# The first layer's mean and variance: from VectorE's statistics to two ScalarE passes

## The chip, the cores and the metric

The kernel runs on one core of a Trainium2 chip. Its time is the device time of one execution in microseconds. Three runs of the kernel before took 1981.17, 1981.98 and 1983.0 us; the median is 1981.98 us.

## The reference, cut to what matters

`x` has 128 batches of 128 rows (graph nodes) and 512 columns, in fp32, and `adj` is a 128 x 128 matrix. Four layers follow each other, and each ends in a layer norm over the 512 columns:

```python
def _layernorm(x, eps=1e-5):
    m, v = mean(x), var(x)          # over the 512 columns
    return (x - m) / sqrt(v + eps)

x = _layernorm(x + norm_adj @ x @ W0 + bias)                        # layer 0
x = _layernorm(x + L1(x, adj, adj, b))                              # layer 1
x = _layernorm(x + ((adj.T * (x Wq.T)(x Wk.T).T) / row norm) @ (x Wv.T))   # layer 2
h = x @ W3                                                          # layer 3
att = softmax(leaky_relu(s1 + s2.T) * adj)
x = _layernorm(x + elu(att @ h + beta * h))
```

Layer 1 is given the same matrix twice. With A equal to C - b, the maximum over all pairs adds to each row only a constant that its layer norm takes away, so that the kernel has no step for this layer's product; what is left of its norm is a factor for the variance of layer 0, `(1 + eps) * var + eps * eps`.

## The kernel before, in words

The work goes in 32 groups of four batches. A group's `x` is 128 rows by 4 x 512 columns. Per group there are these products on PE (all fp32): `y` (x transposed times the normalized adjacency, 16 matmuls), `w` (y times W0), `z` and `v` (x times Wq Wk and x times Wv), `r` (z times x), `f` (the masked relation times v), `k` (x times W3) and `h` (the attention times k). The products `w`, `z`, `v` and `k` use a scheme of seven block products instead of eight (class `Product`); some of the seven use it once more inside: these are first made in four small matmuls (for example step `z1`), then PE needs ACT to copy a part (`bz1`, `before`, L739) and DVE to add (`ez1`, `between`, L743), then come three more (`z18`). Others are added onto a PSUM bank after ACT has copied out what stood there (`cz1`, then `z6`; `cz6`, then `z7`).

The layer norms of layers 0, 2 and 3 are called `w`, `v` and `k`. For `v` and `k` the sum of a row comes with the last update of `x` on DVE; `mean` (L994) turns four sums into the two columns needed, `square_of` (L1000) is an ACT pass with a row sum of squares, `guard` (L1017) adds epsilon on ACT, `scale` (L1012) makes the power -1/2 on POOL, and `apply` (L1027) normalizes on ACT. For `w`, `stats` (L961) runs `bn_stats` and `bn_aggr` on DVE for each batch (steps `stw0` to `stw3`), and `guard` also negates the mean.

Left operands need transposed `x`. DVE transposes blocks of 32 (`xt`, `nt`: `square`, L670), then `xd` and `nd` move the blocks by 16 DMAs issued on SP (`exchange`, L676, issue at L680). The relation and the attention go through DRAM (`across`, L700): one DMA out (`wr`, `aw`), and four back (`cr`, `cat`). On POOL run the sums of left operands (`sy`, `sx`, `sn`: `Left.sum`, L613; the small ones `ly`, `lx`, `ln`: L631), the bias (`bi`, L955), the powers and parts of the softmax.

Everything is issued in an order written out by hand as three lists of step names, with a group number relative to a base: `HEAD` (L110) for the first groups, `TURN` (L258), which is repeated 14 times and moves on by a group each time, and `TAIL` (L275). Within an engine instructions run in the list's order. A turn has parts of six groups: for example group base + 4 is in its `w` product while base + 3 is in `z` and base + 1 in `k`. Buffers are chosen by the table `SLOTS` (L47): one digit for each tile that is made, for the six PSUM banks and the tags of SBUF tiles.

Of the kernel before, what the change touches and what calls it, by code (L numbers as in the profile page):

```python
# [38 lines left out]
AF = mybir.ActivationFunctionType  # L39
# [9 lines left out]
        "012345012345013324015345231455124240510435012532245312312023543413421402402052145230142402"  # L49
        "405233100340153013205320521340135305355234252351453524503210430454115310512125312305211451"  # L50
        "412523102304253042541105305015021541030340351405232432352315320142424230314525325435403451"
        "025252541243050250302310324152525234530121521015041053425252503201454254142134120352525210"
        "514323523435403451025252541243050250302310324152525234530121521015041053425252503201454254"
        "142134120352525210514323523435403451025252541243050250302310324152525234530121521015041053"
        "425252503201454254142134120352525210514323523435403451025252541243050250302310324152525234"
        "530121521015041053425252503043201513105140152035033042453510140541524513202020314220445020"
        "545523405212550033235143024014515313210213142055015354151041043201425125523020130023054354"
        "2045151501250312315415401340132145131523152403145324501324051324051"
    ),
    "S": (  # L60
        "012345601326054321502461532143250123654012106425231064104632501462035142560413524651203546"
        "413406524103561463205164231534062135410216534012605403216504352651403256124320651423046145"
        "320641563062145360231534062135410216534012605403216504352651403256124320651423046145320641"
        "563062145360231534062135410216534012631450326154036413652014326504152602324316052432560324"
        "152630645016325064152306"
    ),
    "l1": (
        "010111010101010010101011001101001011010010110100101101001011010010110100101101001011010010"
        "110100110010110011010110100100110"
    ),  # L70
    "l2": (
        "010101010101010010110110110110110110110110110110110110110110110110110110110110110101110101"
        "01"
    ),
    "C": (
        "010101010101011010101011011011011011011011011011011011011011011011011011011011011011011010"
        "10101010"
    ),
    "aT": (
        "012100212102102012012102012102012102012102012102012102012102012102012102012102102012012010"  # L80
        "2110210"
    ),
    "m": (
        "012301202302301210320100130133212013131201310310213231201012103232120131323021213103232120"
        "131323021213103232120131323021213103232120131323021213103232120131323021213103232120131323"
        "02121310233221302022132020213201210312121203210030"
    ),
    "x": (
        "0123457869789012345768901234576890123457689012345768901234576981032"
    ),  # L90
    "q": (
        "010101010101010001001010101010101010101010101011010101010101010100101010101001010101010101"
        "010101010101010001010101010101010101010101010101010101010101010101010101010101010101010101"
        "010101010101010101010101010101010101010101010101010101010101010101010101010101010101010101"
        "010101010101010101010101010101010101010101010101010101010100010101010101010101010101010101"
        "01010101010101010101010101010101010101010101010101010101010101010101010"
# [14 lines left out]
0.ld1 2.ld0 0.ld0 2.ld1 1.ld1 1.ld0 s.warm s.deg s.root s.nadj s.adjt s.nadjT 0.y10 0.y01 0.cy10  # L111
1.y10 0.cy01 1.y11 1.cy10 1.y01 1.cy11 0.y11 s.m012_0 1.cy01 3.ld1 s.s00 0.w2 s.m012_1 0.cy11
s.s02 0.bi10 s.m012_3 0.y00 0.bi01 2.y10 s.s01 0.cy00 2.y11 0.bi00 0.w1 s.m05_0 0.sy0 s.s03 2.y00
1.y00 0.bi11 s.m05_1 1.cy00 0.sy2 s.m012_2 0.w5 1.bi10 s.m05_3 0.sy3 0.dw1 s.m05_2 0.w6 0.sy1
0.dw2 s.sk0 1.ly12 s.sk2 s.g1 0.dw6 s.s30 0.w7 s.cg1 1.sy0 s.m312_0 1.bi11 0.dw7 s.m312_1 0.w4
1.bi00 0.dw5 s.bi 0.w3 s.sa1 2.cy10 0.dw4 2.cy00 s.sk1 2.cy11 s.g2 s.sa0 0.dw3 0.stw3 3.y11 1.bi01
0.stw0 s.g5 0.stw1 s.sa2 s.dg2 2.y01 s.s31 1.sy2 0.stw2 1.w2 2.cy01 s.s33 s.g6 0.gw s.sa3 1.bw2
s.m35_0 1.w1 s.cg6 0.pow 1.ew2 s.g7 1.bw1 s.m35_1 2.bi11 1.ew1 0.apw0 0.apw1 1.w28 0.xt0 1.ly5
1.w18 s.cg7 s.sk3 s.la 0.apw2 0.apw3 1.sy1 1.w5 1.dw1 3.ld0 0.xt2 s.g4 1.bw5 0.xt1 2.bi01 0.xt3
s.q11 1.w6 2.bi00 s.cg4 0.xd 1.ew5 s.mg12_0 3.bi11 1.w58 s.dg5 s.q02 s.g3 2.bi10 1.dw6 1.dw2 1.w7  # L120
s.dg3 2.ly12 s.mg12_1 1.dw7 s.mg12_3 1.w4 s.sg0 1.dw5 s.sg2 2.w2 s.sg1 4.ld0 2.w1 s.m312_3 2.bw2
s.sg3 2.ew2 2.bw1 0.z1 0.sx0 s.vt3 s.vt0 0.sx2 s.vt1 2.w28 0.cz1 1.dw4 1.sy3 s.vt2 0.z6 1.stw3
s.vd 0.sx1 1.stw2 1.w3 0.cz6 0.sx3 s.mg4_0 2.sy0 0.z5 2.ew1 1.dw3 2.sy1 0.z7 s.mg4_1 2.ly5 1.stw1
2.w18 s.mg4_3 0.cz7 0.z2 2.sy2 0.dz5 1.stw0 0.z4 0.dz2 1.gw s.mg5_0 s.mg12_2 1.pow s.mg5_2 0.z3
0.cz4 s.mg5_1 s.m35_3 1.apw3 s.mg5_3 3.y10 2.dw1 1.apw2 s.sv0 0.v1 1.apw0 3.bi10 2.dw2 1.apw1
1.xt2 s.sv1 0.v2 0.cv1 1.xt3 0.dz3 0.v6 1.xt0 0.dv2 1.xt1 0.r0 s.sv3 0.cv6 1.xd s.mv5_0 2.w5
s.mv4_0 s.mv5_1 s.mv4_1 s.sv2 0.r1 2.bw5 s.mv4_3 s.mv12_0 0.r2 2.ew5 0.r3 s.mv12_2 s.mv12_1 2.w58
s.mv5_3 s.mv12_3 0.rm 0.v7 s.q10 0.sq0 0.rt 0.sq1 2.w6 0.sq2 s.q12 0.cv7 s.q03 0.sq3 s.q00 0.rp
0.v4 s.q13 0.v5 3.cy11 s.q01 3.cy10 0.wr 2.dw6 0.cv4 4.ld1 3.sy0 s.wt0 s.s32 2.w7 2.sy3 0.cr 0.dv5
s.wt1 s.mv5_2 3.y00 1.sx0 2.dw7 0.v3 s.mg4_2 3.cy00 1.lx12 2.dw5 2.w4 s.mv4_2 0.dv3 0.f3 2.dw4  # L130
3.sy1 0.f1 2.stw2 0.f2 3.bi00 2.stw3 1.v1 0.fa3 1.lx4 0.fa2 1.z1 1.bv1 0.fa1 2.w3 1.bz1 1.ev1
1.lx5 1.ez1 0.f0 1.sx2 1.v5 2.dw3 0.fa0 1.z18 1.sx3 1.bv5 2.stw0 1.v18 0.mnv 1.cz1 1.ev5 1.z5
1.sx1 0.qv2 1.z6 2.stw1 0.qv1 1.cv1 0.qv0 1.z2 1.cz6 1.v6 1.bz2 0.qv3 1.ez2 1.bz5 1.z7 0.gv 2.gw
1.ez5 0.pov 1.cv6 2.pow 1.z28 0.apv3 1.z4 1.cz7 1.dz2 0.apv0 1.z58 0.nt3 2.apw0 1.v2 0.sc00 2.apw2
0.nt0 3.y01 1.bz4 0.sc01 0.apv2 1.v58 3.bi01 1.ez4 3.cy01 1.v7 0.apv1 0.nt2 3.ly5 2.apw1 0.sc10
1.bv2 1.z48 2.apw3 0.nt1 1.v4 1.cv7 3.ly12 1.dz4 0.nd 1.ev2 3.w5 1.bv4 1.dz5 1.v28 3.bw5 0.sc11
1.z3 3.ew5 1.dv2 3.w1 0.sc20 3.w2 1.dz3 3.bw1 0.sc21 3.w58 3.ew1 1.r0 1.r1 0.sc30 3.bw2 1.ev4 1.r2
1.r3 3.ew2 1.v48 0.sc31 3.w18 1.dv4 3.w28 0.pw 3.dw1 1.rm 0.k2 0.sn0 3.dw2 1.sq0 2.xt1 1.sq1 0.sn2
0.pe 2.xt0 0.k1 1.sq2 2.xt2 1.sq3 0.sn3 2.xt3 0.k5 1.rt 0.ck1 2.xd 1.rp 1.dv5 s.m312_2 0.sn1 0.pl3
0.dk2 1.v3 0.pl0 s.m35_2 0.pl1 0.pl2 3.sy2 0.k6 1.dv3 0.ej 3.w6 0.ck6 3.sy3 0.ei 0.ex0 0.k7 3.dw6  # L140
0.ex3 0.ex2 0.ex1 3.w7 0.rd 0.ck7 0.so0 0.dk5 0.so1 4.y11 3.dw7 1.wr 0.k4 3.dw5 4.bi11 0.at 0.aw
2.lx12 3.w4 4.cy11 1.cr 0.ck4 3.w3 3.dw4 2.sx0 3.stw2 0.cat 2.z1 3.stw3 2.sx2 2.z2 3.dw3 2.bz1
3.stw0 1.f2 2.sx1 2.bz2 3.stw1 2.v1 2.lx5 2.ez2 1.f0 3.gw 0.k3 1.fa2 2.bv1 3.pow 1.fa0 2.ez1 1.f1
2.lx4 3.apw0 0.dk3 1.f3 3.apw3 3.xt0 3.apw1 2.z18 1.fa1 3.apw2 0.h0 1.fa3 2.cz1 2.v5 3.xt2 1.mnv
3.xt1 0.h3 1.qv0 2.ev1 2.z28 1.qv1 2.z6 3.xt3 1.qv2 2.dz2 3.xd 1.qv3 0.em3 2.v18 0.em0 2.bv5 1.gv
0.h1 2.cz6 2.ev5 1.pov 0.ee0 2.z7 0.ee3 0.em1 1.apv3 0.ea0 1.apv0 0.ea3 2.v58 2.cz7 2.z5 1.sc00
0.ee1 1.apv1 4.y00 1.sc01 2.bz5 0.ea1 4.y10 1.apv2 4.bi00 2.ez5 4.cy00 4.y01 4.cy10 4.bi10 1.sc10
0.h2 4.cy01 1.sc11 2.z4 4.bi01 2.cv1 0.em2 2.v2 1.sc20 2.bz4 4.sy0 0.ee2 2.z58 2.ez4 2.bv2 2.v6
4.ly12 2.ev2 1.nt1 2.z48 2.cv6 1.sc21 2.v28 2.dz4 2.sx3 2.v7 1.sc30 3.sx0 2.dz5 4.w1 1.sc31 2.cv7
3.lx12 2.dv2 2.z3 1.pw 4.bw1 1.nt2 4.ew1 2.v4 2.dz3 1.pe 4.w18 3.sx2 1.nt0 2.bv4 2.r0 1.nt3 3.lx5  # L150
4.dw1 2.r1 2.ev4 3.z2 4.sy2 0.ea2 2.r2 1.pl3 1.pl0 2.r3 4.sy1 0.mnk 1.pl2 4.w6 1.pl1 3.sx1 2.rm
0.qk3 2.rt 2.sq0 1.ej 2.v48 0.qk2 2.wr 4.dw6 3.z1 2.dv4 1.nd 2.sq1 3.lx4 0.qk1 4.w7 1.ei 2.dv5
3.bz1 1.ex0 3.ez1 1.ex1 2.v3 1.ex3 4.sy3 1.ex2 4.dw7 2.sq2 3.bz2 1.rd 2.sq3 1.so0 3.z18 3.ez2
0.qk0 4.w4 3.sx3 3.cz1 2.dv3 0.gk 1.so1 3.z5 4.dw4 3.z6 0.pok 3.bz5 3.ez5 2.rp 0.apk3 3.z28 3.cz6
# [253 lines left out]
def kernel(  # L408
# [43 lines left out]
    def wide(t):  # L452
        return t.rearrange("p a b -> p (a b)")
# [954 lines left out]
```

## Time and profile before

| | |
|---|---|
| median of three runs | 1981.98 us |
| the profiled execution's own time | 1983.26 us |
| its span, first to last instruction | 1981.5 us |
| granted TensorE clock, mean | 0.998 |
| ACT passes of `square_of` (L1003) | 248, 721 to 722 ns each, and 188 ns for the row sum's read |
| ACT passes of `apply` (L1029) | 383, 808 ns each |
| `bn_stats` of `w` on DVE (L965) | 128, 677 ns each |
| 16 DMA issues of one `xd` or `nd` on SP | 10.7 to 12.3 us |

The page gives busy time by engine. PE is the matmuls and PEld the loading of their weights, DVE is VectorE, ACT ScalarE, POOL GpSimd, and SP issues the DMAs. A matmul of fp32 here leaves two records. In the chain of waits a row has a start, a length and what ran; in the groups by line, the two numbers after the first bar are busy microseconds and the mean nanoseconds of one, and after the second bar stands the idle time before them and what ended it.

### The profile page before, as it was taken

To read this page: it belongs to the slowest core of one execution; us is meant where nothing else is said; L and a number is where in the kernel's file an instruction comes from. 1 tells how busy PE (TensorE), PEld (TensorE's weight loads), DVE (VectorE), ACT (ScalarE), POOL (GpSimd) and SP (SyncE) were. 2 spreads that over 40 slices of the span, in tenths; PEclk is the share of its full clock that TensorE was granted. 3 is DMA by queue.
4 is the path that set the end of the run, shared out by engine and by line. 5 is a ranking of instruction groups with operands and counts; after the bars stand their busy time and mean duration, and the time that the engine had idled before them with its cause. 6 is when DMAs were issued, how large, how long until landed. Compare 5 with 4: busy or idle time off the path is not lost.

```text
span 1981.5 us, 37439 instructions
## 1 busy us (share of the span) xinstructions
PE 1954.1 (99%) x12405; PEld 1723.5 (87%) x12405; DVE 1645.2 (83%) x3801; ACT 1125.0 (57%) x2800; POOL 1372.1 (69%) x1702
## 2 busy tenths in 40 slices
PE   8999999999999999999999999999999999999997
PEld 7888988888888988888988888988889888898885
DVE  7888787888788888888888888888888888787887
ACT  2245556565655656565556556556656556566467
POOL 7557678676687776786766776766877767777652
PEclk9999999999999999999999999999999999999999
DMA  5523455334444345444345443445343454434434
GB/s 199 85 52 66 96 80 135 60 87 101 106 100 95 66 89 107 104 99 76 81 91 113 98 106 58 92 98 112 92 102 59 92 106 100 96 62 107 76 73 107
DMA packets 737312, 184.55 MB, mean 93 GB/s; under 512 B 689376, under 2 KB 689760, under 8 KB 737120
## 3 DMA queue, kind: packets, MB, share of 16 engines
q1 hardware_dynamic: 736976, 182.03, 43.7%
q8 instruction: 100, 1.64, 0.4%
q14 instruction: 92, 0.75, 0.1%
q10 hardware_dynamic: 144, 0.13, 0.0%
HBM read 64.03 MB, written 49.87 MB: 57 GB/s over the span
## 4 chain that ended last, share of the span: by engine, by line
PE 86%; SPq 4%; POOL 3%; DMA 2%; DVE 2%; ACT 1%; issue 1%; POOLq 0%; DVEq 0%; ACTq 0%
PE p_w L766 10%; PE p_k L766 10%; PE p_v L730 9%; PE p_z L730 8%; PE p_v L766 8%; PE p_z L766 8%; PE p_w L730 7%; PE p_k L730 6%; PE pr L1142 5%; PE pl_k L1190 5%; PE pl_v L1190 5%; PE py L935 5%; SPq L680 4%; POOL x L585 1%; PE pk L1059 1%
## 5 line engine op out<-in xcount | busy, mean ns | idle before, releaser
L1029 ACT ACTIVATE x<-x,nb,r 128x512 f32<-128x512 f32 x383 | 289.6, 808 | 28.8 <-POOL nb L585 28.5
L585 POOL TENSOR_TENSOR x<-x,bias_bc 128x512 f32<-128x512 f32 x128 | 165.7, 1299 | 122.0 <-PE py L935 92.3
L588 POOL TENSOR_TENSOR r<-v,minus_half 128x4 f32<-128x4 f32 (+1 forms) x99 | 99.1, 1001 | 200.8 <-ACT v L1025 189.5
L582 DVE TENSOR_TENSOR x<-p_w,x 128x512 f32<-128x512 f32 x224 | 153.6, 686 | 48.4 <-PE p_w L766 22.3
L1214 DVE SCALAR_TENSOR_TENSOR e<-x,wa_bc 128x512 f32<-128x512 f32 x256 | 172.3, 673 | 1.4 <-ACT x L1029 0.7
L579 ACT COPY C_k<-p_k 128x512 f32<-128x512 f32 x124 | 71.7, 579 | 150.0 <-PE p_k L766 137.5
L935 PE MATMUL py<-nadjT,x 128*128 128x128 f32 x1024 | 134.8, 277 | 1.0 <-DVE x L1310 0.6
L935 PEld LDWEIGHTS py<-nadjT,x 128*128 128x128 f32 x1024 | 126.9, 193 | 5.1 <-issue 1.4
L1190 PE MATMUL pl_k<-C_k,attT 128*128 128x512 f32 x248 | 122.9, 594 | 1.8 <-DMA attT<-d_a 1.7
L1190 PE MATMUL pl_v<-C_v,relT 128*128 128x512 f32 x248 | 121.0, 593 | 0.9 <-DMA relT<-d_r 0.9
L766 PE MATMUL p_z<-S_x,gq 128*128 128x256 f32 x512 | 121.3, 380 | 0.2 <-DVE C_z L582 0.2
L766 PE MATMUL p_w<-w,S_y 128*128 128x256 f32 x512 | 121.2, 379 | 0.4 <-DVE x L582 0.4
L766 PE MATMUL p_v<-wvT,S_x 128*128 128x256 f32 x512 | 121.1, 379 | 0.0
L1305 ACT ACTIVATE pl_k<-pl_k 128x512 f32<-128x512 f32 x127 | 73.4, 581 | 80.3 <-DVE x L1302 79.4
L766 PE MATMUL p_k<-w,S_n 128*128 128x256 f32 x496 | 117.3, 379 | 0.0
L1199 DVE SCALAR_TENSOR_TENSOR x<-pl_v,r,x 128x512 f32<-128x512 f32 x128 | 94.7, 746 | 23.9 <-PE pl_v L1190 18.9
L582 DVE TENSOR_TENSOR p_z<-p_z,q_z 128x128 f32<-128x128 f32 x248 | 107.3, 433 | 8.5
L582 DVE TENSOR_TENSOR p_v<-p_v,q_v 128x128 f32<-128x128 f32 x248 | 107.3, 433 | 8.5
L766 PEld LDWEIGHTS p_z<-S_x,gq 128*128 128x128 f32 x512 | 94.2, 190 | 21.2 <-issue 6.9
L582 DVE TENSOR_TENSOR C_v<-p_v,C_v 128x512 f32<-128x512 f32 x127 | 86.5, 681 | 28.9 <-ACT C_v L579 13.5
L766 PEld LDWEIGHTS p_w<-w,S_y 128*128 128x128 f32 x512 | 93.2, 190 | 12.2 <-issue 1.1
L766 PEld LDWEIGHTS p_k<-w,S_n 128*128 128x128 f32 x496 | 91.6, 190 | 14.0 <-issue 2.9
(1627 smaller groups left out, 6246.6 us busy)
## 6 DMA issues: line engine op xcount, KB each, us to landing
x<-in_x_dram SPq DMA_DIRECT2D x64, 512.0 KB, 4.5
out_dram<-x SPq DMA_DIRECT2D x127, 256.0 KB, 2.5
d_r<-ru SPq DMA_DIRECT2D x31, 256.0 KB, 2.0
relT<-d_r SPq DMA_DIRECT2D x124, 64.0 KB, 2.5
s<-d_s SPq DMA_DIRECT2D x31, 256.0 KB, 3.8
d_a<-au SPq DMA_DIRECT2D x31, 256.0 KB, 2.3
attT<-d_a SPq DMA_DIRECT2D x124, 64.0 KB, 4.0
w<-in_L_gnn_weight_dram SPq DMA_DIRECT2D x1, 1024.0 KB, 9.5
```

The costliest lines, as they stand in the source:

```text
L582: nc.vector.tensor_tensor(o, a, b, f)
L585: nc.gpsimd.tensor_tensor(o, a, b, f)
L588: nc.gpsimd.tensor_tensor(o, v, minus_half[:, : v.shape[-1]], ALU.pow)
L680: nc.sync.dma_start(out=o[rows(to), :, :, rows(q)], in_=self.u[rows(q), :, :, to])
L730: nc.tensor.matmul(self.banks[i][:, r, bass.ts(c, P)], lhsT=lhsT, rhs=rhs, start=(not then and n == 0), stop=(n == len(steps) - 1), skip_g ...
L766: nc.tensor.matmul(ps[:, j, :], lhsT=lhsT, rhs=rhs, start=(i not in ONTO and j == 0 and kc == 0), stop=(j == 1 and kc == 1), skip_group_ch ...
L935: nc.tensor.matmul(o, lhsT=self.x_chunk(b, kc), rhs=nadjT, start=True, stop=True)
L1029: nc.scalar.activation(xt, xt, AF.Identity, bias=self.nb[k][:, b : b + 1], scale=self.rstd[k][:, b : b + 1],)
L1142: nc.tensor.matmul(self.pr[:, b, :], lhsT=self.whole["z"][:, fc, b // 2, bass.ts(b % 2, P)], rhs=self.xT.chunk(b, fc), start=(fc == 0), st ...
L1190: nc.tensor.matmul(ps, lhsT=left[:, b, :], rhs=self.whole[k][:, b, :], start=True, stop=True)
L1199: nc.vector.scalar_tensor_tensor(xt, self.pf[b], self.rnorm[:, b : b + 1], xt, ALU.mult, ALU.add, accum_out=self.total("v", b),)
L1214: nc.vector.scalar_tensor_tensor(wide(self.e), self.x(b), 1.0, wide(wa_bc[k]), ALU.mult, ALU.mult, accum_out=self.s[:, k, b : b + 1],)
```

## The change

For layer 0 the statistics on DVE (`stw0` to `stw3`) go. In their place each batch has a step `suw`, an ACT pass that writes `x` onto itself with a row sum, and a step `qw`, the square pass with a row sum, as for the other layers; between them stands one `mnw` (`mean`) for each group. The square pass writes its unused output onto the group's transposed `y`. The lists of steps and the table of slots are new ones throughout: `HEAD` has 2397 steps instead of 2332, `TURN` 245 instead of 240, and `TAIL` 2066 instead of 2041. All other steps are the same ones, in another order. The core of the diff, with the part of `TURN` around the layer 0 steps:

```diff
 TURN
-... 4.dw5 2.qv3 3.ez1 3.lx4 2.gv 1.k7 4.dw4 4.stw2 2.pov 3.z18 4.stw3 1.ck7 3.z2 3.sx3 3.cz1 1.dk5 2.apv1 1.k4 ...
-... 4.w3 3.bv2 2.sc01 3.ev2 3.z28 4.dw3 1.k3 3.dz2 4.stw1 3.z4 4.stw0 3.v1 1.dk3 4.gw 1.dk2 3.bz4 3.z7 4.pow ...
+... 4.dw5 3.sx2 2.qv1 3.ez1 2.gv 1.k7 3.lx4 4.dw4 4.suw2 3.z18 2.pov 4.suw3 3.z2 1.ck7 3.sx3 4.w3 2.apv3 ...
+... 2.apv0 4.dw3 3.cz1 2.nt2 3.bz2 3.v2 2.nt0 4.suw1 2.sc00 3.z6 1.ck4 3.ez2 3.bv2 4.suw0 2.sc01 3.z4 4.mnw
+3.cz6 3.ev2 3.z28 4.qw2 1.k28 2.sc10 3.bz4 4.qw1 3.z7 3.ez4 2.nd 4.qw3 1.dk2 4.qw0 1.k3 3.dz2 3.cz7 2.sc11 4.gw 4.pow ...
@@ small
-            bufs = 4 if tag in ("r", "nb", "nm", "v") else 2
+            bufs = 4 if tag in ("r", "nb", "nm", "v") else 3 if tag == "sum" else 2
@@ after mean
+        def sum_of(self, k, b):
+            nc.scalar.activation(self.x(b), self.x(b), AF.Identity, accum_out=self.total(k, b))
+
+        def junk(self, k, b):
+            if k == "w":
+                return self.y.aT[:, b].rearrange("p a n -> p (a n)")
+            return wide(self.relT if k == "v" else self.attT)
@@ square_of
-                wide(self.relT if k == "v" else self.attT),
+                self.junk(k, b),
@@ guard
-            if k == "w":
-                self.var_[k] = self.small("v")
-                self.nm[k] = self.small("nm")
-                nc.scalar.mul(self.nm[k], self.mv[k][:, :, 0], -1.0)
-                v, bias, f = self.mv[k][:, :, 1], eps_bc[:, 1:2], 1.0 + EPS
-            else:
-                v, bias, f = self.var_[k], eps_bc[:, 0:1], 1.0
+            v = self.var_[k]
+            bias, f = (eps_bc[:, 1:2], 1.0 + EPS) if k == "w" else (eps_bc[:, 0:1], 1.0)
@@ step
+            elif kind == "suw":
+                self.sum_of("w", *n)
-            elif kind in ("qv", "qk"):
+            elif kind in ("qw", "qv", "qk"):
```

In the first 100 us the list of `HEAD` also has the sums `0.sy0` and `0.sy2` ahead of the first bias step, where before `0.bi10`, `0.bi01` and `0.bi00` stood ahead of `0.sy0`.

## The prediction

> **What bounds the kernel now.** I read the page's first two parts, then the stretches (busy time by engine in five windows), then the chain of waits, then the waits of PE, then the groups by line.
>
> ```profile
> span 1981.5 us, 37439 instructions
> PE 1954.1 (99%) x12405; PEld 1723.5 (87%) x12405; DVE 1645.2 (83%) x3801; ACT 1125.0 (57%) x2800; POOL 1372.1 (69%) x1702
> ```
>
> ```profile
> 660.00:1500.00 840.00, 840.00 (x5430) 745.75 (x5429) 707.93 (x1638) 494.23 (x1232) 607.75 (x758) 1.00 0.45 93
> ```
>
> The columns of the second are the window, its length, and busy time of PE, PEld, DVE, ACT and POOL. PE has no idle time at all in 840 us, in which the same turn of steps repeats. The chain gives the pace there:
>
> ```profile
> 349.96 1.73 PE p_z L766 x8
> ...
> 855.81 2.68 PE pr L1142 x24
> ...
> 915.88 2.68 PE pr L1142 x24
> ```
>
> Eight 256-column matmuls take 1.73 us (0.216 each), 24 of 128 columns 2.68 (0.1117), and the same step returns every 60.07 us. A group of four batches needs per turn, by these paces (0.43 for a 512-column one), y 3.57, w 11.6, z 11.43, v 11.43, k 11.6, r 3.57, f 3.44, h 3.44 = 60.1 us. So a steady turn is PE's own work and nothing else.
>
> Over the whole trace I counted the matmuls by shape: 8115 x 0.1116 + 3771 x 0.2159 + 518 x 0.4293 = 1942 us. Before the first matmul lie 1.4 us, after the last about 12 us. The remaining 25.7 us are time between starts beyond the pace: 15.2 up to the first attention-like product of group 0 (at 105.3 us), 3.0 at the end of the list, the rest nearly all between 106 and 660 us. The waits of PE name them:
>
> ```profile
> PE p_w L766 <- DVE x L582: 3.8, 4, 1.7
> PE pl_k L1190 <- DMA attT<-d_a: 1.7, 2, 1.4
> ...
> PE p_z L766 <- DMA x_0T<-sq_x: 1.2, 1, 1.2
> PE pl_v L1190 <- DMA relT<-d_r: 0.9, 1, 0.9
> ```
>
> Here a rule has to be weighed. The page's row says LDWEIGHTS busy 87%. The Trainium skill ("Perfetto Trace Analysis", section Identifying the Most-Contended Engine) says to judge headroom by MFU and LDWEIGHTS share, not by matmul occupancy. By that there would be 258 us of headroom, and 5% from any lighter engine would be thinkable. The pace says otherwise: 39 us in all (1981.5 - 1942), of which some 13 are the two ends. I take the pace, because the turn is exactly as long as its matmuls.
>
> **The change, part by part.**
>
> ```profile
> L1003 ACT ACTIVATE attT<-x,neg 128x512 f32<-128x512 f32 x124 | 89.5, 721 | 1.4
> L965 DVE BATCH_NORM_STATS2 st_w<-x 128x6 f32<-128x512 f32 x128 | 86.7, 677 | 1.0
> ...
> L1003 ACT ACTIVATION_READ_ACCUMULATOR attT<-x,neg 128x1 f32 x124 | 23.4, 188 | 0.0
> ...
> L966 DVE BATCH_NORM_AGGREGATE mv_w<-st_w 128x2 f32<-128x6 f32 x128 | 23.3, 182 | 4.4
> ...
> L1021 ACT ACTIVATE nm<-mv_w 128x4 f32<-128x4 f32 x32 | 6.6, 206 | 73.3 <-DVE mv_w L966 73.2
> ```
>
> Removed from DVE: 128 x (677 + 182) ns = 110 us, so 1535 of busy time (77%), 3.4 us a turn. Removed from ACT: 32 small instructions, 6.6 us. Added to ACT: 128 square passes, which exist already for the other layers, at 721 + 188 ns = 116 us; 128 row-sum passes, unseen so far, between that 721 and the 808 ns of the normalizing pass (same function, two column operands), plus the 188 read: 116 to 128 us; 32 pairs of `mean` at 207 + 193 ns = 13 us. ACT comes to about 1370 us (69%), 7.4 us more a turn. Both functions run already, and the trace has one table load in all, so no table is switched.
>
> The second rule speaks against this: "ScalarE: Activation LUTs", Rules for kernel authors, puts add and multiply on VectorE. The rows agree that it is dearer (1.8 us a batch on ACT for 0.86 on DVE). If ACT's or DVE's time counted, the rule's sum would be +130 us and the other engine's -110; as 60.07 us of PE cover both DVE's 50.5 and ACT's 35 to 42 us per turn, both sums are hidden and the price is 0 in a steady turn, provided that no PE step comes to wait behind the burst of passes.
>
> *The steady turn.* In the new list the passes stand between PE offsets 20 and 35 us of the turn, among the copies that free PSUM for PE. Tightest are the copies of z1 and z6. Worked out from durations of before: lx12 can start at offset 12.8 (its transposed operand lands 13.5 us after the first of 16 DMA issues, as in before: 806.11 to 819.59), then on POOL lx12 2.9, three sums 3.7, lx4 1.8, power and product 1.2: 22.4. ACT's four normalizing passes at 0.76 spacing end at 25.4, the copy of z1 at 26.0; z6 is due at 26.6. Then bz2, suw1, ck4, bv2, suw0, mean: 28.8, the copy of z6 29.4; z7 is due at 30.6. Slack 0.6 and 1.2 us. In before I measured slack per wait of PE: apart from one of 0.08 the smallest in a turn were 0.67 to 0.8. So nothing is lost, but the first has little to give. The DVE steps lose work only.
>
> *The start.* PE work ahead of the first z product (waiting for group 0's transposed x) is 48.9 us before and 47.2 in the new list. In before x was ready at 63.5 through: last update of x 36.8, statistics and queue to 42.2, power, normalize, transpose to 50.5, 16 DMA issues 10.85 us, landing 2.3. New: the sums of y go ahead of the bias that waits 10.1 us for its DMA on POOL, so PE's early waits for DVE and POOL shrink and the last update stays at 36 to 37; then sums 1.7, means 0.25, squares 3.4, copies 1.0, guard 0.2, power 1.2, other copies 1.0 to 2.0, normalize 3.0, transpose 0.7: 49 to 51, that is x at 62 to 63.5. PE is there with 1.7 us less work done and up to 1.5 earlier: +1.0 (range -1 to +2).
>
> *Waits for DMA later.* The lists are in order of execution (before's 16-DMA steps start where the list has them, within a microsecond), so I compare PE work between a DMA step and its first consumer. relT needs 7.4 us (97.94 to 105.31) and gets 6.1 in group 2 (+1.3) and 6.6 in group 7 (+0.8). attT had 6.4 and 7.3 in groups 5 and 6, waited 1.6 and 0.5, and now gets 8.6 and 25.8 (-2.1). n of group 0 had 11.3, waited 0.7, and gets 12.8 (-0.7). n of the last group had 10.0, waited 0.5, and gets 8.6 (+1.4). Sum +0.7. The number of DMAs is unchanged, and SP's order around them moves with these steps.
>
> *Waits for DVE and ACT.* After 106 us PE lost 5.0 us to late DVE and 1.8 to late ACT (each with about 0.1 for the restart). DVE's could stay (0) or vanish (-5.0): with 7% less work I take half, -2.5. ACT's could stay (0) or triple (+3.7), as its load rises by a fifth and comes in bursts: +2.2, a little past double. Second small products need 1.83 us after the first (measured: 2.62 apart left 0.79 slack), and three in the new list have 1.53, 1.73 and 1.75: +0.5. Sum +0.2, between -5 and +4.
>
> *The end.* The last h products are followed by the same maximum, exponential, sum, statistics, power, normalize and DMA; PE's last start to the end stays 12 us, within 0.5.
>
> Sum against the profiled execution (1983.26 us, span 1981.5): +1.0 + 0.7 + 0.2 = +1.9, so 1985.2 for a profiled one. The median shown, 1981.98, is 1.3 below the profiled run's own time; against it 1983.9. What a measurement of this kernel can tell from no change is about 0.2%, 4 us: 1978 to 1986.
>
> **The rivals.** *No bound is touched* (my forecast, 0.48): turns stay at 60.07 and only start and end shuffle, 1983.9, itself between 1978 and 1986 or a little beyond.
>
> *The lighter DVE pays* (0.17): DVE's 5.0 us of PE waits vanish, the attT and n gains come and ACT costs nothing: 1982 + 1.0 - 2.1 - 0.7 - 5.0 + 1.3 = 1976.5. For it: PE's largest named wait is for DVE. Against it: in the 840 us window DVE costs PE nothing, so the gain is bounded by the ramp and the end.
>
> *Copies late behind the row sums* (0.35, slower): z6 (or k6 of the turn's beginning, 0.7 us by the same layout) waits for a PSUM copy on ACT, because the four normalizing passes start only after POOL's power, and the row sums share the queue. Each microsecond beyond 0.6 of slack costs PE that time in each of 25 full groups. It decides from 0.1 us of wait per group (2.5 us on top of +1.9 reach the limit). With POOL's chain 1.1 us later, 0.5 lost: 1983.9 + 12.5 = 1996. For it: ACT would be busy without a break from offset 20 to 38. Against it: POOL and ACT ran up to 0.8 us ahead of the list in before's turn.
>
> That the change doesn't do what it says is excluded: 128 of DVE's 133 statistics are gone from the built program.
>
> **Numbers.** 1983.9. Below, the DVE rival with half a microsecond to spare gives 1976; above, half a microsecond per turn in most groups gives 1994. Under 1976 and over 1994 I leave about 2 in 10. Faster 0.17, same 0.48, slower 0.35.
>
> **What would show it.** Right: PE busy for the whole of 660 to 1500 us; the same step 60.07 us apart in the chain; ACT near 1370 and DVE near 1535; the first z at 62 to 64 us; relT waits of about a microsecond in groups 2 and 7, none for attT of groups 5 and 6. Wrong: a p_z or p_k wait on an ACT copy that returns every turn (slower rival), PE waits for DVE gone everywhere after 106 us (faster rival), or a first z more than 2 us away from 63.5. What I cannot see from before is how late ACT runs in the ramp; an error of several microseconds there would break the forecast without a rival being right.

## The result and the profile after

The changed kernel takes 1993.44 us (median, 1992.8 to 1995.04) against 1981.64 beside it: ratio 1.0059, 95% interval 1.0043 to 1.0075. It is slower by more than 0.2%. The forecast was 1983.9; its range held the time, but its likeliest case, no change, did not come true. The first two lines of the page, the fourth of the five windows, and three steps of the chain of waits:

```profile
span 1991.2 us, 37591 instructions
PE 1958.6 (98%) x12405; PEld 1724.9 (87%) x12405; DVE 1555.0 (78%) x3545; ACT 1293.4 (65%) x3344; POOL 1367.6 (69%) x1702
```

```profile
660.00:1500.00 840.00, 840.00 (x5427) 745.98 (x5427) 663.71 (x1524) 568.05 (x1469) 602.25 (x756) 1.00 0.45 93
```

```profile
740.08 2.68 PE pr L1150 x24
800.15 2.68 PE pr L1150 x24
860.22 2.68 PE pr L1150 x24
```

ACT has 168 us more, DVE 90 us less, and in the repeated turn neither matters: PE is busy for all of the 840 us and the same step returns every 60.07 us, as before. So the whole loss lies outside. I took each matmul's start, the next one's start and the pace of its shape (0.1116, 0.2159, 0.4293 us), and summed what lies between two starts beyond the pace:

| us beyond the pace | 0 to 106 | 106 to 660 | 660 to 1500 | 1500 to the end | sum |
|---|---|---|---|---|---|
| before | 14.8 | 7.5 | 0.3 | 3.1 | 25.7 |
| after | 14.4 | 13.3 | 0.0 | 10.7 | 38.4 |

That is 12.7 us more. The spans differ by only 9.7, mostly because 9.3 us lie behind the start of the last matmul where 12.0 lay before. The ramp to the steady turn (106 to 660 us) loses 5.8 us and the run-out (from 1500 us on) 7.6. The waits of PE name much of it:

```profile
PE p_w L771 <- DVE x L587: 4.2, 3, 1.8
PE pl_v L1198 <- DMA relT<-d_r: 3.8, 3, 3.3
PE p_k L735 <- DVE p_k L587: 2.7, 3, 2.2
PE p_k L771 <- ACT C_k L584: 1.7, 2, 1.0
...
PE p_z L735 <- POOL l_x L590: 1.2, 1, 1.2
```

The columns are the waits' sum, their number and the longest. The first line lies wholly before 106 us and stood in before too (3.8). Each of the others is mainly one long wait or two, in one place, not a short one that returns. The waits for attT of before are gone, as forecast.

*The longest, at 220 us.* SP's own instructions, which issue the DMAs, and then PE:

```profile
199.51 12.62 SPq L685 DMA_DIRECT2D n_1T<-sq_n  x16
212.23 0.57 SPq L708 DMA_DIRECT2D d_r<-ru  x1
...
214.85 2.61 SPq L712 DMA_DIRECT2D relT<-d_r  x4
```

```profile
216.82 0.39 PE L735 MATMUL p_z<-l_x,gq_t 128*128 128x128 f32 x2
220.52 3.75 PE L1198 MATMUL pl_v<-C_v,relT 128*128 128x512 f32 x4 [3.31 <-DMA relT<-d_r]
...
226.53 1.88 PE L1198 MATMUL pl_v<-C_v,relT 128*128 128x512 f32 x4
```

The source of the write, ru, was ready at 202.3 (DVE's transpose of 0.70 us begins at 201.62), but SP was in the middle of n_1T's 16 issues. The new list has `1.nd` ahead of `2.wr`. In before SP had this order, and PE did not wait:

```profile
201.41 0.32 SPq L703 DMA_DIRECT2D d_r<-ru  x1
202.31 10.71 SPq L680 DMA_DIRECT2D n_1T<-sq_n  x16
213.12 3.33 SPq L707 DMA_DIRECT2D relT<-d_r  x4
```

There the read stood behind n_1T too, and relT landed at 218.53, only 1.9 us earlier than after (220.43). PE came to the product at 219.43; in the kernel after it was free for it at 217.2. So the wait comes from both: a write and read that lie behind the 16 issues, and a PE that has 2.2 us less to do until then. The second fence shows a further price: the same four 512-column matmuls take 3.75 us after the wait and 1.88 at 226.53. PE works at half pace for some 5.7 us (its granted clock is 0.50 there), so a wait of 3.3 costs about 3 more.

*The run-out.* POOL and SP around 1800 us, then PE:

```profile
1804.36 1.27 POOL L590 TENSOR_TENSOR S_x<-x_29T 128x512 f32<-128x512 f32 x1 [16.51 <-DMA x_29T<-sq_x]
```

```profile
1791.11 11.68 SPq L685 DMA_DIRECT2D x_29T<-sq_x  x16
```

```profile
1812.26 0.71 PE L735 MATMUL p_z<-l_x,m_g 128*128 128x128 f32 x4 [1.20 <-POOL l_x L590]
1814.00 0.46 PE L735 MATMUL p_z<-x_29T,gq 128*128 128x128 f32 x2 [0.81 <-DVE p_z L587]
```

x_29T is issued at 1791.11, when PE's last small v product of group 28 has let go of a transposed-operand buffer (SP's waits name it: 4.7 us for PE p_v); in before its 16 issues ran from 1772.98 to 1784.29. POOL stands still for 16.5 us, and its sums of group 29 come too late for PE.

### The profile page after: what moved, and what is told of

It is laid out like the page before. It is cut to its first block, busy times and chain, and to the rows that moved or that the text cites. A ratio compares the mean times of both kernels' runs of the same rounds, so it can differ in the third digit from the quotient of the medians.

```text
span 1991.2 us, 37591 instructions
## 1 busy us (share of the span) xinstructions
PE 1958.6 (98%) x12405; PEld 1724.9 (87%) x12405; DVE 1555.0 (78%) x3545; ACT 1293.4 (65%) x3344; POOL 1367.6 (69%) x1702
## 4 chain that ended last, share of the span: by engine, by line
PE 83%; POOL 5%; SPq 5%; DVE 3%; DMA 2%; ACT 2%; issue 1%; ACTq 0%; POOLq 0%; DVEq 0%
PE p_k L771 9%; PE p_w L771 9%; PE p_v L735 9%; PE p_z L735 9%; PE p_z L771 8%; PE p_v L771 7%; PE p_w L735 6%; PE p_k L735 6%; PE pl_v L1198 5%; PE pr L1150 5%; PE pl_k L1198 4%; PE py L940 4%; SPq L685 4%; POOL x L590 1%; ACT x L1037 1%
## 5 line engine op out<-in xcount | busy, mean ns | idle before, releaser
L584 ACT COPY q_w<-p_w 128x256 f32<-128x256 f32 x93 | 34.1, 367 | 145.9 <-issue 97.7
L1006 ACT ACTIVATE x<-x 128x512 f32<-128x512 f32 x128 | 80.1, 626 | 59.1 <-DVE x L587 58.9
```

The costliest lines, as they stand in the source:

```text
L584: nc.scalar.copy(o, i)
```

## The experiments

**Theory A:** the passes cost nothing; the new order costs the time, where DMA steps and close pairs of products stand in ramp and run-out. **Theory B:** ScalarE's 168 us more make it late there, whatever the order.

### The passes alone, in the order of before

```
 TURN: 4.stw2 .. 4.stw0 -> 4.suw2 .. 4.suw0 4.mnw 3.v1 1.dk3 4.qw2 1.dk2 3.bz4 4.qw3 3.z7 3.bv1 4.qw1 2.sc10 3.ez4 4.qw0 4.gw 4.pow
 junk("w"): y.aT -> a bf16 tile of its own; "nm" 3 buffers for 4
```

> The order of the kernel before, with the passes alone: each bn_stats pair on VectorE becomes a row sum on ScalarE at the same place, and the four squares follow the last of them, one after every second step, with guard and power behind them (the squares' unread output goes into a small tile of its own, so that no buffer is held longer). Theory A (the new order costs the time, at its two ends; the passes cost nothing): the PE has no new wait in the repeated turn (60.1 us a turn) and no 3.5 us wait at 220 us, so 1980 to 1986. Theory B (ScalarE's added 168 us make it late in the ramp and at the end, whatever the order): 1990 or more, with matmuls waiting on ScalarE's copies.

Measured: 2050.04 us, ratio 1.0337 (1.0323 to 1.0351). A's range falls. B's holds, matmuls do wait for ScalarE's copies; but they wait in the repeated turns as well, which neither theory had. Window and waits of PE there:

```profile
660.00:1500.00 840.00, 819.85 (x5252) 724.73 (x5252) 642.40 (x1474) 552.31 (x1420) 582.14 (x731) 1.00 0.44 90
```

```profile
PE py L937 <- ACT C_z L581: 13.2, 14, 0.9
PE p_z L732 <- DVE p_z L584: 7.0, 14, 0.5
```

Fourteen turns have the same two waits. In the longer one y's bank comes free with a C_z copy on ScalarE, and ScalarE and PE show why the copy is late:

```profile
933.02 0.81 ACT L1034 ACTIVATE x<-x,nb,r 128x512 f32<-128x512 f32 x1 [1.41 <-POOL nb L587]
933.74 0.57 ACT L581 COPY C_z<-p_z 128x512 f32<-128x512 f32 x1
```

```profile
934.36 1.16 PE L937 MATMUL py<-nadjT,x 128*128 128x128 f32 x8 [0.94 <-ACT C_z L581]
```

The copy queues behind a normalizing pass that waits for POOL's power, and the power now comes after four squares (guard and power also stand later in this list). ScalarE is idle for 1.41 us just before, so what is too long is the chain, not ScalarE's load. The turn is 62.01 us (pr at 945.79 and 1007.80), 1.94 more. The passes are not free by themselves: an order made without them has no room where they land. That is the mechanism of my slower rival, in a kernel that I had not forecast. The turns from 660 to 1500 us hold 27 of the 67 us; the rest lies in ramp and run-out.

### The old statistics in the new order

```
-TURN: 4.suw2 4.suw3 .. 4.suw1 .. 4.suw0 .. 4.mnw .. 4.qw2 4.qw1 4.qw3 4.qw0 .. 4.gw
+TURN: 4.stw2 4.stw3 .. 4.stw1 .. 4.stw0 .. 4.gw          (HEAD, TAIL alike)
```

> The order of the kernel after, with VectorE's statistics in the place of the row sums and without the squares. A: what the order does to the transfers stays: f of group 2 still waits about 3.5 us for relT behind n_1T's 16 issues and runs on at half pace, and z of group 29 still waits for x_29T, so 1988 to 1994. B: the added ScalarE work is gone, so back to 1980 to 1984.

Measured: 2025.57 us, ratio 1.0213 (1.0200 to 1.0227). B falls: less ScalarE work is slower. A's number falls too, since the new order has no room for VectorE's statistics: its turns now have a wait of p_z for DVE (0.4 us; pr at 940.78 and 1001.46, 60.68 apart), and 106 to 660 us hold 28.8 us beyond the pace for 13.3.

### No statistics at all, in the new order and in the old

```
 sum_of: accumulate -> once a group: nc.gpsimd.memset(self.sum_[k], 0.0)
 square_of("w"): Square pass -> once a group: nc.gpsimd.memset(self.var_[k], 1.0)
```

> The kernel after with neither statistics nor passes for the first layer: sums and variances are constants (set once a group on GpSimd), so the first layer's mean and variance are left out. ScalarE has 168 us less, VectorE no more than after. A: the order's waits for relT of group 2 and x_29T stay, 1987 to 1994. B: 1977 to 1984.

Measured: 1995.78 us, ratio 1.0063 (1.0050 to 1.0077), level with the kernel after (1.0059); that is 1.8 us over A's range and far from B's. This is the run that decides. With all 168 us of ScalarE gone, ScalarE stands idle for 4.4 us at 268 us, just before group 3's squares, and PE still waits as in the kernel after:

```profile
PE pl_v L1204 <- DMA relT<-d_r: 4.3, 2, 3.9
PE p_w L771 <- DVE x L587: 4.3, 3, 1.9
PE p_k L735 <- DVE p_k L587: 2.6, 2, 2.4
PE p_k L771 <- ACT C_k L584: 1.7, 2, 1.0
```

```
 stats("w"): bn_stats, bn_aggr -> once a group: nc.gpsimd.memset(self.mv[k], 1.0)      (kernel before)
```

> The kernel before without the first layer's statistics: mean and variance are constants (set once a group on GpSimd), so the first layer's mean and variance are left out, 120 us of VectorE. It bounds what any move of that work away from VectorE could bring in the order of before. If VectorE is off the path (A): 1978 to 1984. If VectorE's load was a part of what held the kernel before: under 1975.

Measured: 1982.47 us, ratio 0.9996 (0.9987 to 1.0004). The statistics on VectorE cost nothing in before, so in this order no move of them could have gained anything. And with the first layer's statistics left out of both kernels, the new order alone still costs 13 us (1995.78 against 1982.47). The window has DVE at 668.51 for 707.93, and PE at the same 840.00:

```profile
660.00:1500.00 840.00, 840.00 (x5430) 745.50 (x5429) 668.51 (x1528) 491.96 (x1232) 606.47 (x770) 1.00 0.45 93
```

### More ScalarE work in the new order

```
+for _ in range(2 if k == "w" else 1):     # the other: 2 if k == "w" and b == 0
     nc.scalar.activation(self.junk(k, b), self.x(b), AF.Square, ...)
```

> The kernel after with every first-layer square made twice (the second writes the same again): some 0.8 us more per row block, 3.3 us of ScalarE more a turn and 105 us in all. A (ScalarE has room in the repeated turn, its bulk isn't the price): the turn stays at 60.07 us, and the ends lose 0 to 4 us: 1993 to 1998. B (ScalarE's load sets the loss): as much again as the passes took, 2000 or more, with waits on ScalarE in the turn.

Measured: 2050.40 us, ratio 1.0332 (1.0318 to 1.0346). A's forecast of room in the turn falls, and the time is in B's range (2000 or more, with waits in the turn). Window and PE's waits in it:

```profile
660.00:1500.00 840.00, 829.84 (x5278) 728.03 (x5277) 647.12 (x1493) 595.22 (x1536) 582.47 (x734) 1.00 0.44 92
```

```profile
PE p_z L735 <- DVE p_z L587: 6.1, 14, 0.4
PE py L940 <- DVE C_z L587: 3.4, 14, 0.2
```

ScalarE is at 71% of the window, PE at 99%, and yet each turn waits. Beyond the pace lie 20.9 us in 14 turns, so a turn is 61.57. ScalarE's work in a turn is 595.22 x 61.57 / 840 = 43.6 us for 40.6 in the kernel after: 3.0 us more cost 1.5. The waits are for VectorE by name, but in the longer one VectorE itself waits for a ScalarE copy behind the doubled squares (`bz5`, ahead of the product z58). The other 36 of the 57 us lie outside the window.

> The kernel after with one of the four first-layer squares of a group made twice: 0.8 us more of ScalarE a turn, 26 us in all. If ScalarE has some room in the repeated turn: the turn stays at 60.07 us and the time at 1992 to 1996. If it is at its limit there (four extra squares cost 1.5 us a turn): 0.3 to 0.4 us a turn, and with the ends a quarter of the 57 us that four cost, 2003 to 2010.

Measured: 1996.18 us, ratio 1.0070 (1.0058 to 1.0083). ScalarE at 576.51 in the window, 41.2 us a turn: 0.6 us more, and 0.9 us beyond the pace in all 14 turns. So the turn has room for 0.6 us of ScalarE, at a busy share of 69%, and not for 3.0. The ramp has less: in the profiled execution, the slowest of five (2000.19), 106 to 660 us hold 18.1 us beyond the pace for 13.3.

### Mending the order

```
 HEAD: 1.nd 2.dv4 .. 2.wr .. 2.cr 1.so1 -> 2.dv4 .. 2.wr .. 2.cr 1.nd 1.so1
```

> The kernel after with one step moved: n_1T's 16 issues go behind relT's write and read of group 2 on SP. A: relT is issued some 10 us earlier, the 3.5 us wait at 220 us and the 2.9 us that the PE loses at half pace after it go, and nothing else waits for n_1T before 225 us: 6.4 us less, 1986 to 1989. B (ScalarE is late there anyway): the wait goes to another operand, 1991 to 1995.

Measured: 1990.15 us, ratio 1.0036 (1.0023 to 1.0048); the profiled spans are 1988.0 for 1991.2. SP and PE there:

```profile
202.59 0.33 SPq L704 DMA_DIRECT2D d_r<-ru  x1
...
205.19 2.61 SPq L708 DMA_DIRECT2D relT<-d_r  x4
207.89 12.60 SPq L681 DMA_DIRECT2D n_1T<-sq_n  x16
```

```profile
217.37 1.88 PE L1194 MATMUL pl_v<-C_v,relT 128*128 128x512 f32 x4
...
225.46 0.71 PE L731 MATMUL p_k<-m,l_n 128*128 128x128 f32 x4 [1.36 <-POOL l_n L586]
```

The relT wait and the half pace behind it are gone: 180 to 240 us hold 2.45 us beyond the pace for 7.18. But about half of the 6.4 us that A forecast comes back. n_1T lands later, so POOL's l_n is late for k of group 1 (1.36). And 240 to 300 us hold 5.02 for 3.39, since PE now runs at half pace after k18's wait of 2.2 us, which stands in both kernels; the last section comes back to this. The intervals of this kernel and the kernel after overlap a little; the traces show the cause.

```
 HEAD: 2.k2 4.gw 3.qv3 2.k1 4.pow 2.cat 2.bk2 1.h3 3.qv0 2.ek2 2.sn2 4.apw3 1.em3 2.bk1 .. 2.ek1
    -> 2.k2 2.bk2 2.ek2 4.gw 3.qv3 2.k1 2.bk1 2.ek1 4.pow 2.cat 1.h3 3.qv0 2.sn2 4.apw3 1.em3
```

> The kernel with relT's way first, and ScalarE's copies of group 2's small k products (with VectorE's sums behind them) moved to just behind the products, ahead of the guard, squares and applies that they were queued behind. A (each wait is a place in the order): the 2.35 us wait of k18 at 268 us there goes to about 0.4, and the PE's half pace behind it (about 2 us) with it: 1990.15 less 3.5 to 4.5, 1985.5 to 1987. B (ScalarE as a whole is late there): the wait only moves to the next copy, 1989 to 1991.

Measured: 1991.22 us, ratio 1.0039 (1.0026 to 1.0051): no gain. PE at the place:

```profile
269.72 0.46 PE L731 MATMUL p_k<-w,n_2T 128*128 128x128 f32 x2 [0.25 <-DVE p_k L583]
...
271.88 0.49 PE L731 MATMUL p_w<-w,y_5T 128*128 128x128 f32 x2 [1.25 <-DVE x L1314]
```

k18's wait shrinks as A said, and the next product waits in its stead: w1 of group 5 needs a bank that the exps of group 1's h products, late on ScalarE, still hold. Here B's words were right, and the time is within 0.3 us of its range: the wait moved on.

```
 HEAD: 3.z3 3.dz3 ahead of 1.k2; 1.k18 behind 3.r1; 4.bz4 behind 4.z4
 TAIL: 7.v4 ahead of 6.k58, 7.v48 ahead of 9.w5; 10.z1 ahead of 7.k6; 8.h0 ahead of 9.k4; 9.ck7 ahead of 9.ex2
```

> The same with five more local moves of single steps: z3 of group 3 ahead of k of group 1 and k18 of group 1 two steps later; z4's copy of group 4 ahead of pl of group 3; v4 and v48 of group 28 a step or two earlier (x_29T's buffer comes free sooner); z1 of group 31 ahead of k6 of group 28; h0 of group 29 and the C_k copy of group 30 ahead of k4. A: each takes its wait away (1.5, 1.1, 0.9 to 1.8, 0.8 and 0.9 us of the PE), so 5 us less than without them: 1980 to 1983, level with the kernel before. B: 1987 to 1992.

Measured: 1994.40 us, ratio 1.0054 (1.0042 to 1.0067), above the ranges of both. h0 of group 29 waits 3.7 us for its bank and z1 of group 31 1.5 us; l_n's wait is gone.

```
 as above without 10.z1 and 8.h0; HEAD: 1.ee2 1.ee1 ahead of 4.gw; 5.cr ahead of 4.cat
```

> The kernel with relT's way first and the k copies moved, and single moves chosen again from the last traces: z3 of group 3 ahead of k of group 1 and k18 of group 1 behind r1; z4's copy of group 4 ahead of pl of group 3; the exps of group 1's first two h products ahead of the guard of group 4 (their banks are what w1 of group 5 then waited 1.4 us for); relT's read of group 5 ahead of attT's read of group 4; v4 and v48 of group 28 a step earlier; the C_k copy of group 30 ahead of two exps. Without the moves of h0 and z1 that had cost 3.8 and 0.8 us. If the loss is a sum of places in the order that can be mended one by one: 1984 to 1987. If each wait only moves to the next operand of an order that is too tight there: 1988 to 1992.

Measured: 1990.95 us, ratio 1.0040 (1.0026 to 1.0053), with 36.4 us beyond the pace for 35.1 with relT's move alone. The time is in the range of the second of the two theories put down for it, and the waits fit it: k18 waits 1.23 us again and w1 of group 5 1.08. None of these versions beats the kernel before.

## Why the prediction was wrong in its likeliest case

The time lies inside the range, 0.6 us below its top, and that is luck: the top stood for half a microsecond lost in most turns, and no turn lost anything. What the prediction said that it could not see, how late ACT runs in the ramp, is a part of what came.

- *What bounds it, and the LDWEIGHTS rule set aside:* right. Without the statistics the kernel before is 0.04% faster, within its interval; of the rule's 258 us of headroom nothing showed, and the faster rival falls with it.
- *DVE 1535, ACT 1370:* 1555 and 1293. Two terms were mis-sized. One is the row sums. I put them between 721 and 808 ns; the groups by line after:

```profile
L1006 ACT ACTIVATE x<-x 128x512 f32<-128x512 f32 x128 | 80.1, 626 | 59.1 <-DVE x L587 58.9
...
L1006 ACT ACTIVATION_READ_ACCUMULATOR x<-x 128x1 f32 x128 | 24.3, 190 | 0.0
...
L1016 ACT ACTIVATE relT<-x,neg 128x512 f32<-128x512 f32 x124 | 89.5, 721 | 2.0
```

  My neighbours had one and two column operands, the row sum has none: 626, 721, 807 ns are a step of some 90 each. The Trainium skill ("ScalarE: Activation LUTs", section What ACT_TABLE_LOAD costs) gives 186 ns + 0.833 ns a column without and 93 more for each such operand, so by estimate 613, near the trace. I should have extrapolated the rows. The larger term is overlap: in the traces the records of one engine overlap, and the page counts such time once. One by one ACT's records add up to 1298.8 us before and 1523.5 after, 224.7 more for the 245 of my sum, while the busy time rises by 168; DVE's fall by 103, its busy time by 90. In the window that is 5.3 us more of ACT a turn, for my 7.4.
- *The steady turn costs nothing:* right, at 60.07 us. The slack of "0.6 and 1.2 us" was near: in the kernel after the two C_z copies end 1.0 to 1.1 us ahead of z6 and 1.45 us ahead of z7. The room that the doubled squares measure is another one, that of z58.
- *The start, +1.0:* measured -0.4 up to 106 us beyond the pace, with the first z at 62.9. Right within its range, but not in its parts: PE's waits for DVE up to there grew from 5.1 to 6.9 us, where I had them shrink, and those for DMA fell from 2.4 to 1.4.
- *Waits for DMA later, +0.7:* this step failed first. For relT of group 2 I wrote that it "needs 7.4 us (97.94 to 105.31) and gets 6.1", +1.3. The 7.4 are from group 0, where the write went out undelayed. In group 2 the list puts n_1T's 16 issues ahead of the write, 12.62 us of SP; I noted that "SP's order around them moves with these steps" and priced nothing for it. From the write, at 212.23, PE had 5.0 us of work and needed 8.3. It waited 3.3 us, and the half pace made it about 6. attT's gain came as forecast; of the 1.4 for the last group's n came 1.0 (a wait of 1.3 for 0.3), which the trace puts down to DVE, since n had landed 0.4 us before it ended; group 7's wait did not come.
- *Waits for DVE and ACT, +0.2:* failed. Three close pairs of small products were to cost 0.5; group 2's k18 alone waited 2.2, since the copy between stood behind other ScalarE steps; their spacing on PE was only one of the two conditions. That VectorE's waits after 106 us would halve (5.0 to 2.5) was wrong too: PE's named waits for DVE there are 1.3 us before and 5.6 after. The largest group before, 3.8 us of w products, lies ahead of 106 us. Those for ACT went from 0.7 to 2.8, near the forecast growth.
- *The run-out* had no term at all beyond n of the last group, and lost 7.6 us: buffers handed over later (x_29T) and C_k copies behind other ScalarE work.
- *The end stays within 0.5:* it became 2.8 us shorter, 9.3 from PE's last start for 12.0.
- *The slower rival:* it would be slower by a copy late in every turn. It is slower, but by single waits outside the turn, and not by ScalarE's load: without it they stay. The rival's mechanism is real, as the passes in the old order and the doubled squares show; the new order keeps clear of it.

So the cause is shown to be the new order's ramp and run-out: with neither passes nor statistics in it, the loss stays (1.0063). Which order would carry the passes without it stays open: of four hand-made repairs the best got 3 us of 12 back. A run-out repaired from x_29T's buffer on was not found, so that what is said of its causes rests on the waits in the trace alone.

## What to carry to other kernels

An order made for one mix of work is part of the kernel: the same passes cost 67 us where I put them into the old order, and 12 in one made for them. When a list is new, price its ramp and run-out step by step, with each DMA queue as an engine of its own: what is issued between a write and its read, and how long. And before moving work off an engine, run the kernel without that work: here it would have said that in this order there was nothing to gain.

## What the runs showed of the hardware

After a wait PE can run at half pace for a while, and the granted clock shows it. These are windows of the kernel after; in each the column ahead of the last two is the clock:

```profile
220.50:226.20 5.70, 5.68 (x15) 3.62 (x16) 2.13 (x5) 0.00 (x0) 1.00 (x2) 0.50 0.00 0
227.00:232.00 5.00, 5.00 (x36) 4.26 (x35) 4.20 (x11) 2.17 (x8) 1.02 (x2) 1.00 0.01 2
```

After a wait of 3.3 us PE works at half pace for 5.7 us, after 3.9 us (no statistics, at 222 us) for 2.9, after 2.2 us (relT's way first, at 270 us) for 3.6, and in the kernel after, behind a wait of 2.2 us at 275 us, not at all. By the trace's clock record each such stretch lasts 3.41 us or twice that (219.6 to 226.4 us in the kernel after). The Trainium skill ("TensorE: Matmul & The Clock Gate", Part 1: The HAM clock gate) tells of a half clock after an idle window of about 3.4 us that runs free. The length agrees, but the window need not be idle: an estimate from the starts and their pace, over the clock records of all twelve traces between the first 12 us and the last matmul, is that PE had work for 0 to 38% of the 3.41 us ahead of each fall, and that no stretch of this grid with 39% or more brought one. The grid also tells the two waits of 2.2 us apart: at 270 us it lay in one stretch, which was left with 23% of work; at 275 us it was split over two, with 44% and about 71%.
